# Stencil products over a chunk border by 32x32 corners, and another order of the first batches, in a four-layer kernel

## The chip, the cores and the metric

The kernel runs on one core of a Trainium2 chip. The metric is the device time of one execution in microseconds. A core has TensorE (PE; its weight loads are shown apart as PEld), VectorE (DVE), ScalarE (ACT), GpSimd (POOL) and SyncE (SP), which here only issues transfers. Each works through its own list of instructions in order and waits at semaphores for the others. Matmuls write to PSUM, which has eight banks of 128 rows x 512 f32; all else lives in SBUF, with 128 rows (partitions). A dimension of 256 is held as two chunks of 128 rows.

## The reference

Sixteen batches of a 256 x 256 array x pass through four layers, all f32.

```python
# 0: adapter with an expert chosen per batch, then layer norm
h = gelu(x @ down_W.T + down_b); h = h @ Wsel.T + bsel + emb
x = LN(h @ up_W.T + up_b + x) * gamma + beta
# 1: attention with 16 heads under a bias, a mask, a timestep's scale and shift; then a feed-forward
h = LN(x) * (1 + scale) + shift
x = h + softmax(q k^T / 4 + bias, mask) v @ Wo + bo
x = x + gelu2(LN2(x) @ W1 + b1) @ W2 + b2
# 2: one of three small networks, chosen per batch, then layer norm
x = LN(x + branch(x)) * gamma + beta
# 3: one step of a differential equation on the 256 x 256 grid
df = -(grad(A0*x, 1) + grad(A1*x, 2)) \
     + 0.5*(grad2(B0*x, 1) + grad2(B1*x, 2) + 2*grad(grad(B2*x, 2), 1))
x = max(x + df * dt, 0)
```

(The shift, scale and normalisations are as written in the usual way; the two mixed terms of layer 3 are equal.) `grad` is a central difference, `grad2` a second difference, each one-sided at the two outer rows or columns. So as a 256 x 256 matrix each has entries beside its diagonal and a few more in its first and last row.

## The kernel before

Everything of a batch stays on the chip from its first load to the output. The program is written out for all 16 batches, with no loop on the device, as nine generators ("chains"): `adapt` (layer 0, two batches at a time), `prepare` (its layer norms), `project` (q, k, v), `weigh` (scores and exponentials), `attend`, `enter` and `feed` (feed-forward), `end` (layer 2) and `step` (layer 3).

A planner, `Flow`, decides in which order their instructions are put into the engines' lists. A chain yields the time at which it can go on, or a condition on what other chains have done. `Flow` keeps a clock for each engine from fixed costs (`flow.pe(1.35)` adds 1.35 us to TensorE's), and takes, of the chains that are ready, the one with the lowest due time. A chain's due time begins at the number given to `flow.add` and grows with the TensorE time that it spends. The costs and due times only set the order: on the chip only semaphores count. Seven PSUM banks are shared among all chains (`misc` takes one, `free` gives it back), one is kept for the attention's context.

**Layer 3** (`step`). For a batch, `f` is the normalised array and `e_t` its transpose in PSUM. DVE and POOL multiply them by the grids: `b2_`, `a1`, `b1_` from the transpose, `a0`, `b0` from `f`. `e_z` is the first difference of `b2_` along the columns and is added to `a0`. Then `e_d` sums five products, for one output chunk `c` after the other, each in a bank of its own: the second difference along rows, `h_m` times `b0` (line 1128, two full matmuls, one for each chunk `k` of rows); the differences along columns of `a1` and `b1_` (line 1131, four matmuls of 129 columns, since from a chunk the matrices reach only one column beyond it); and the first difference along rows, `g_m` times `a0` (line 1135, two full matmuls). DVE then makes `f + dt * e_d` (line 1137), ACT applies the maximum (line 1145), SP stores. Matrices `g_m` and `h_m` hold the differences. For `k` other than `c`, only the entries next to the border between the two chunks are not zero: a corner of the 128 x 128 block.

**The start.** Constants are loaded from ACT's queue (`load`), the first inputs from SP's. Pair 0 passes `adapt`: `p_h` (line 543), Gelu to `a_h` (line 547), `p_e` with the expert's weights `e_w` (line 558), `p_u` (line 574) and the addition to `x` (line 580). POOL has first spread the mask (line 382) and added a bias to `x` (`biased`, line 529). `prepare` takes statistics (lines 417 to 425, on DVE and POOL), normalises, takes statistics again, and normalises once more to `c_ln` (line 433). `project` transposes `c_ln` to `c_t`, scales it on ACT and computes q, k and v with `w_qkv` (lines 646 and 689). `weigh` begins with the mask's product (line 733). `idle` (line 222) puts matmuls of zeros where TensorE has nothing else to do.

Of the kernel before, what the change touches and what calls it, by code (L numbers as in the profile page):

```python
# [170 lines left out]
def chain_kernel(ctx: ExitStack, tc: tile.TileContext, t: dict, out: bass.AP):  # L171
# [19 lines left out]
    def chunked(w):  # L191
        return w.rearrange("(k p) n -> p k n", p=P)
# [173 lines left out]

    rows_a = load("rows_a", rows(t["rows_a"]), [P, 5 * D])
    ln0_g, ln0_b, bv, bo, up_b = (rows_a[:, i * D : (i + 1) * D] for i in range(5))
    w_qkv = load("w_qkv", chunked(t["W_qkv"]), [P, NC, 3 * D])
    wq, wk, wv = (w_qkv[:, :, i * D : (i + 1) * D] for i in range(3))  # L370
    bqz = fixed("bqz", [P, NC])
    nc.vector.tensor_scalar(bqz, bq, columns("odd"), None, ALU.mult)
# [160 lines left out]
    def adapt():  # L533

        for p in range(B // 2):
            yield lambda: p in e_ws
            yield arrives.get(("t", p), 0.0)
            parts = [slice(i * A, (i + 1) * A) for i in range(2)]
            w, xt = e_ws.pop(p), xts.pop(p)
            ps_h = misc(f"p_h{p}", [2 * A, S])  # L540
            for k in range(NC):
                for i in range(2):
                    nc.tensor.matmul(
                        ps_h[parts[i]], w_down[:, k, :], xt[:, i, k, :], start=k == 0, stop=k == NC - 1
                    )
            h1 = xp.tile([2 * A, S], F32, name=f"a_h1{p}", tag="a_h1", bufs=1)
            nc.scalar.activation(h1, ps_h, AF.Gelu, bias=columns("down_b"))
            at = free(f"p_h{p}", flow.act(0.47, flow.pe(1.0), "gelu"))
            if p == 0:
                expert_bias()  # L550
            yield at
            if p == 0:
                spread_mask(0)
                for b in range(2):
                    biased(b)
            ps_e = misc(f"p_e{p}", [2 * A, S])
            for i in range(2):
                nc.tensor.matmul(ps_e[parts[i]], w[parts[i]], h1[parts[i]], start=True, stop=True)
            h2 = xp.tile([2 * A, S], F32, name=f"a_h2{p}", tag="a_h2", bufs=1)
            nc.vector.tensor_scalar(h2, ps_e, e_add[:, p : p + 1], None, ALU.add)  # L560
            at = free(f"p_e{p}", flow.dve(0.4, flow.pe(0.5)))
            if p and 2 * p + 2 < B:
                load_turned(p + 1)
                load_expert(p + 1)
            if p:
                yield lambda: ("x", 2 * p + 1) in done
            yield at, 2
            if p == 0:
                timestep()
                idle(256)  # L570
            ps_u = [misc(f"p_u{2 * p + i}", [P, NC, D]) for i in range(2)]
            for c in range(NC):
                for i in range(2):
                    nc.tensor.matmul(
                        ps_u[i][:, c, :], h2[parts[i], c * P : (c + 1) * P], up[parts[i]], start=True, stop=True
                    )
            at = flow.pe(1.0)
            for b in (2 * p, 2 * p + 1):
                x = xs[b]
                nc.vector.tensor_tensor(x, ps_u[b % 2], x, ALU.add)  # L580
                adapted[b] = free(f"p_u{b}", flow.dve(0.7, at))
                done.add(("adapt", b))
                yield 0.0, 0

    def prepare():
        for b in range(B):
            yield lambda: ("adapt", b) in done
            x, at = xs.pop(b), adapted.pop(b)
            yield at, 0
            flow.spent += 0.75  # L590
            if b + 2 < B:
                load_x(b + 2)
                if b == 0:
                    load_turned(1)
                    load_expert(1)
            if b == 1:
                choose()
            stat, at = take_stats(f"0_{b}", x, at)
            if b == 0:
                condition()  # L600
                idle(512, 512)
            yield at, 0
            tmp = xp.tile([P, NC, D], F32, name=f"b_tmp{b}", tag="b_tmp", bufs=1)
            at = normalized_affine(x, x, stat, ln0_g, ln0_b, tmp, b == 0)
            yield at, 0
            stat, at = take_stats(f"1_{b}", x, at)
            if b == 0:
                conditioned()
                masked.update((m, 0.0) for m in range(4))
            yield at, 0  # L610
            if b > 1:
                yield lambda: ("turned", b - 2) in done
            ln = xp.tile([P, NC, D], F32, name=f"c_ln{b}", tag="c_ln", bufs=2)
            lns[b] = ln, normalized(ln, x, stat, b == 0)
            flow.spent += 1.5
            if b + 2 < B:
                biased(b + 2)
            done.add(("normal", b))

    def project():  # L620
# [464 lines left out]
    def step():  # L1085
# [6 lines left out]
        for b in range(B):  # L1092
            yield lambda: ("branch", b) in done
            y, stat, at = stats3.pop(b)
            yield at, 0
            tmp = wide(f"e_tmp{b}")
            f = y
            yield normalized_affine(f, y, stat, ln3_g, ln3_b, tmp, b == B - 1)
            ps_t = misc(f"e_t{b}", [P, NC, S])
            at = transposed(ps_t, f)  # L1100
            b2_, a1, b1_ = (wide(f"e_{n}{b}") for n in ("b2", "a1", "b1"))
            for dst, grid in ((b2_, b2_g), (a1, a1_g), (b1_, b1_g)):
                nc.vector.tensor_tensor(dst, ps_t, grid, ALU.mult)  # L1103
                at = flow.dve(0.6, at)
            free(f"e_t{b}", at)
            a0, b0 = wide(f"e_a0{b}"), wide(f"e_b0{b}")
            nc.gpsimd.tensor_tensor(a0, f, a0_g, ALU.mult)
            nc.gpsimd.tensor_tensor(b0, f, b0_g, ALU.mult)
            flow.pool(2.7)
            yield at - 1.4  # L1110
            ps_z = misc(f"e_z{b}", [P, NC, S])
            for c in range(NC):
                rng = slice(c * P, (c + 1) * P)
                nc.tensor.matmul(ps_z[:, c, :], b2_[:, 0, rng], g_m[:, 0, :], start=True, stop=False)  # L1114
                nc.tensor.matmul(  # L1115
                    ps_z[:, c, reach[1]], b2_[:, 1, rng], g_m[:, 1, reach[1]], start=False, stop=True
                )
            at = flow.pe(1.35)
            nc.vector.tensor_tensor(a0, ps_z, a0, ALU.add)
            yield free(f"e_z{b}", flow.dve(0.61, at))  # L1120
            if b == B - 2:
                yield lambda: ("branch", B - 1) in done
            o = wide(f"e_o{b}")
            for c in range(NC):
                rng = slice(c * P, (c + 1) * P)
                ps_d = misc(f"e_d{b}_{c}", [P, S])
                for k in range(NC):
                    nc.tensor.matmul(ps_d, h_m[:, k, rng], b0[:, k, :], start=k == 0, stop=False)  # L1128
                for k in range(NC):
                    for src, w in ((a1, g_m), (b1_, h_m)):  # L1130
                        nc.tensor.matmul(  # L1131
                            ps_d[:, reach[k]], src[:, k, rng], w[:, k, reach[k]], start=False, stop=False
                        )
                for k in range(NC):
                    nc.tensor.matmul(ps_d, g_m[:, k, rng], a0[:, k, :], start=False, stop=k == NC - 1)  # L1135
                at = flow.pe(2.6)
                nc.vector.scalar_tensor_tensor(  # L1137
                    o[:, c, :], ps_d, dt[:, b : b + 1], f[:, c, :], ALU.mult, ALU.add
                )
                at = free(f"e_d{b}_{c}", flow.dve(0.4, at))  # L1140
                part = slice(c, c + 1) if b == B - 1 else slice(0, NC)
                if c:
                    done.add(("step", b))
                if c or b == B - 1:
                    nc.scalar.activation(o[:, part, :], o[:, part, :], AF.Relu)  # L1145
                    flow.act(0.54, at)
                    nc.sync.dma_start(
                        out=out[b].rearrange("(c p) d -> p c d", p=P)[:, part, :], in_=o[:, part, :]
                    )
                yield 0.0  # L1150

    flow.add(adapt(), -3.55, 1.2)
    flow.add(prepare(), -2.34, 2.25)
    flow.add(project(), -0.88, 5.7)
    flow.add(weigh(), 0, 21.2)
    flow.add(attend(), 0.96, 11.3)
    flow.add(enter(), -0.11, 0.44)
    flow.add(feed(), 2.45, 13.9)
    flow.add(end(), 2.86, 3.95)
    flow.add(step(), 4.31, 7.0)  # L1160
    flow.run()

def _arrays(inputs):
# [79 lines left out]
```

## Time and profile before

| | |
|---|---|
| median of three runs | 924.78 us (921.94 to 926.36) |
| profiled execution | 923.92 us, its span 922.1 us |
| TensorE busy | 882.4 us (96%), mean granted clock 0.978 |
| DVE, ACT, POOL busy | 627.8, 556.5, 376.6 us |
| first scores on TensorE | 41.39 us |
| last matmul of batch 15's e_d ends | 918.4 us |

A profile line of the timeline gives the start, the length, the engine, the line of the kernel, the operation, what it writes and reads, its shape, and how many records are merged ("x4"); in brackets the idle time of the engine before it and what ended it. "128*128 128x256" is a matmul that uses 128 rows and 128 columns of the array and writes 128 x 256 elements. Matmuls overlap, so the spacing of their starts says what one costs, and not their length. One f32 matmul leaves two records.

### The profile page before, as it was taken

To read this page: it belongs to the slowest core of one execution; us is meant where nothing else is said; L and a number is where in the kernel's file an instruction comes from. 1 tells how busy PE (TensorE), PEld (TensorE's weight loads), DVE (VectorE), ACT (ScalarE), POOL (GpSimd) and SP (SyncE) were. 2 spreads that over 40 slices of the span, in tenths; PEclk is the share of its full clock that TensorE was granted. 3 is DMA by queue.
4 is the path that set the end of the run, shared out by engine and by line. 5 is a ranking of instruction groups with operands and counts; after the bars stand their busy time and mean duration, and the time that the engine had idled before them with its cause. 6 is when DMAs were issued, how large, how long until landed. Compare 5 with 4: busy or idle time off the path is not lost. (4 is left out here: it accounts for less than half of the span.)

```text
span 922.1 us, 18224 instructions
## 1 busy us (share of the span) xinstructions
PE 882.4 (96%) x6180; PEld 692.1 (75%) x6180; DVE 627.8 (68%) x2078; ACT 556.5 (60%) x1561; POOL 376.6 (41%) x514
## 2 busy tenths in 40 slices
PE   7799898999999999999999999999999999999997
PEld 4467585778787787877787778877878778877785
DVE  4477766888576777766767666766777676766443
ACT  2376747766566666766675767666675655656320
POOL 2234526653522425344543636154452525222331
PEclk7699999999999999999999999999999999999999
DMA  9269978876777877778667776777667775850010
GB/s 296 72 218 296 288 190 211 223 186 175 182 195 189 218 178 188 202 182 213 161 181 210 192 184 178 188 187 193 155 183 180 181 200 143 220 135 29 13 41 23
DMA packets 130972, 163.25 MB, mean 177 GB/s; under 512 B 12713, under 2 KB 94779, under 8 KB 130875
## 3 DMA queue, kind: packets, MB, share of 16 engines
q1 hardware_dynamic: 97920, 96.92, 33.1%
q0 software_dynamic: 31680, 62.92, 33.0%
q10 hardware_dynamic: 1275, 2.19, 0.7%
q8 instruction: 52, 0.85, 0.4%
q14 instruction: 45, 0.37, 0.1%
HBM read 94.89 MB, written 4.19 MB: 107 GB/s over the span
## 5 line engine op out<-in xcount | busy, mean ns | idle before, releaser
L767 ACT ACTIVATE c_pr<-c_sc,c_mx 128x256 f32<-128x256 f32 x512 | 254.9, 500 | 165.8 <-DVE c_mx L756 164.7
L756 DVE CUSTOM_DVE_ANT_0 c_sc<-c_s,side 128x256 f32<-128x256 f32 x512 | 193.6, 418 | 34.7 <-PE c_s L738 18.0
L464 PE MATMUL c_pt<-ident,c_pr 128*128 128x128 f32 x1024 | 143.5, 278 | 6.7 <-DVE x L580 2.1
L464 PEld LDWEIGHTS c_pt<-ident,c_pr 128*128 128x128 f32 x1024 | 116.8, 142 | 34.2 <-issue 11.9
L472 DVE COPY c_pts<-c_pt 128x512 f32<-128x512 f32 x175 | 117.2, 685 | 26.8 <-PE c_pt L464 26.5
L922 PE MATMUL d_f<-d_ht,w 128*128 128x256 f32 x512 | 122.3, 382 | 0.4
L421 POOL TENSOR_SCALAR rs<-mv 128x2 f32<-128x2 f32 x64 | 14.2, 222 | 253.2 <-DVE mv L418 252.7
L952 PE MATMUL d_o<-w,d_z 128*128 128x256 f32 x512 | 115.9, 380 | 0.1
L517 POOL DMA_DIRECT2D side<-neg x60 | 80.7, 1345 | 59.5 <-DMA side<-in_side 20.8
L952 PEld LDWEIGHTS d_o<-w,d_z 128*128 128x128 f32 x512 | 94.9, 190 | 12.5 <-DVE c_mx L756 0.6
L922 PEld LDWEIGHTS d_f<-d_ht,w 128*128 128x128 f32 x512 | 92.8, 190 | 15.1 <-issue 2.5
L767 ACT ACTIVATION_READ_ACCUMULATOR c_pr<-c_sc,c_mx 128x1 f32 x512 | 96.3, 188 | 0.0
L738 PE MATMUL c_s<-c_kt,c_qz 32*128 32x256 f32 x1024 | 78.3, 401 | 4.2 <-DVE c_mx L756 3.8
L821 PE MATMUL c_c<-c_pts,c_va 128*32 128x256 f32 x1024 | 72.6, 385 | 2.5 <-ACT c_pts L474 1.8
L738 PEld LDWEIGHTS c_s<-c_kt,c_qz 32*128 32x128 f32 x1024 | 49.1, 184 | 25.2 <-issue 12.2
L474 ACT COPY c_pts<-c_pt 128x512 f32<-128x512 f32 x81 | 45.5, 575 | 21.1 <-PE c_pt L464 21.0
L941 ACT ACTIVATE d_f<-d_z 128x512 f32<-128x512 f32 x64 | 38.4, 600 | 28.3 <-DVE d_z L938 27.2
L821 PEld LDWEIGHTS c_c<-c_pts,c_va 128*32 128x32 f32 x1024 | 27.9, 109 | 35.0 <-issue 18.2
L456 POOL TENSOR_TENSOR b_tmp<-b_tmp,rows_a 128x512 f32<-128x512 f32 x15 | 19.6, 1304 | 84.1 <-DVE b_tmp L433 65.7
L938 DVE TENSOR_SCALAR d_z<-d_f,cols 128x256 f32<-128x256 f32 x88 | 38.5, 479 | 17.3 <-PE d_f L922 17.2
L422 POOL TENSOR_TENSOR rs<-rs,inv_sqrt 128x2 f32<-128x2 f32 x64 | 46.0, 718 | 5.3
L960 DVE SCALAR_TENSOR_TENSOR y<-d_o,y 128x256 f32<-128x256 f32 x32 | 13.6, 424 | 45.4 <-PE d_o L952 45.4
(152 smaller groups left out, 1606.6 us busy)
## 6 DMA issues: line engine op xcount, KB each, us to landing
side<-in_side SPq DMA_DIRECT2D x256, 256.0 KB, 5.3
side<-neg POOLq DMA_DIRECT2D x60, 1024.0 KB, 8.1
d_w<-in_W_branch SPq DMA_DIRECT2D x16, 512.0 KB, 4.4
xt<-in_x_t SPq DMA_DIRECT2D x16, 256.0 KB, 5.2
x<-in_x SPq DMA_DIRECT2D x16, 256.0 KB, 5.9
out<-e_o SPq DMA_DIRECT2D x15, 256.0 KB, 3.9
w<-in_W SPq DMA_DIRECT2D x2, 1024.0 KB, 7.0
d_bout<-in_bl_branch SPq DMA_DIRECT2D x16, 128.0 KB, 4.3
```

What stands on the lines that cost most here:

```text
L422: nc.gpsimd.tensor_tensor(rs, rs, inv_sqrt, ALU.pow)
L464: nc.tensor.transpose(ps[:, k, c * P : (c + 1) * P], src[:, c, k * P : (k + 1) * P], ident)
L472: nc.vector.tensor_copy(dst, ps)
L474: nc.scalar.copy(dst, ps)
L517: nc.gpsimd.dma_start(out=sides[m].rearrange("p (h c) k -> p h (c k)", h=HB), in_=negs[m // 4].rearrange("p c k -> p (c k)").unsqueeze(1). ...
L738: nc.tensor.matmul(ps[i][:, c, :], qz[rows32, par, half, c * P : (c + 1) * P], k_t[rows32, half, :], start=b > 0, stop=b > 0 or c == NC - 1,)
L756: nc.vector.tensor_tensor_reduce(out=sc[:, c, :], in0=ps[i][:, c, :], in1=sb[:, i * NC + c, :], scale=-1.0, scalar=3.0e38, op0=ALU.add, op ...
L767: nc.scalar.activation(pr[:, c, :], sc[:, c, :], AF.Exp, bias=mx[:, c : c + 1], scale=-1.0, accum_out=sums[:, c, h : h + 1],)
L821: nc.tensor.matmul(ps_c[32 * i : 32 * i + 32, :], va[:, k, 4 * half + i, 2 * par : 2 * par + 2, :].rearrange("p e d -> p (e d)"), turned[i ...
L922: nc.tensor.matmul(ps_f[:, i, :], w1[:, k, f * P : (f + 1) * P], h_t[:, k, :], start=k == 0, stop=k == NC - 1,)
L938: nc.vector.tensor_scalar(z[:, i, :], ps_f[:, i, :], b1[:, f : f + 1], None, ALU.add)
L952: nc.tensor.matmul(ps_o, us[f // 2][:, f % 2, c * P : (c + 1) * P], w2[:, f, :], start=f == 0, stop=f == NF - 1,)
```

## The change

In `step`, the two output chunks share one bank `ps_d`. The first step sums what does not depend on `e_z`: each chunk's own block of `h_m` times `b0`, and the differences along columns. After a yield the second step adds four corner products (`next_to`: the last 32 rows of one chunk against the first 32 of the other, a 32 x 32 piece of the array), and each chunk's own block of `g_m` times `a0`. One DVE instruction then takes both chunks; for the last batch, one for each chunk, both behind the last matmul.

In the setup, `w_qkv` is loaded behind the first Gelu on ACT's queue. Pair 1 and later pairs of `adapt` wait for batch 1's last normalisation, and the addition to batch 1's `x` waits for batch 0's. The biases of batches 1 and 2 are added after batch 0's normalisation; batch 0's comes before the mask is spread. The third group of `idle` has four matmuls for two. The planner gets new costs for `step` and new due times.

```diff
-    w_qkv = load("w_qkv", chunked(t["W_qkv"]), [P, NC, 3 * D])
+    w_qkv = fixed("w_qkv", [P, NC, 3 * D])
...
-            yield lambda: p in e_ws
+            yield lambda: p in e_ws and (p == 0 or ("normal", 1) in done)
...
             if p == 0:
+                nc.scalar.dma_start(out=w_qkv, in_=chunked(t["W_qkv"]))
                 expert_bias()
             yield at
             if p == 0:
+                biased(0)
                 spread_mask(0)
-                for b in range(2):
-                    biased(b)
...
             for b in (2 * p, 2 * p + 1):
+                if b == 1:
+                    yield lambda: ("normal", 0) in done
                 x = xs[b]
...
-                idle(512, 512)
+                idle(512, 512, 512, 512)
...
-            if b + 2 < B:
-                biased(b + 2)
+            for n in (1, 2) if b == 0 else (b + 2,) if b + 2 < B else ():
+                biased(n)
...
-            yield free(f"e_z{b}", flow.dve(0.61, at))
+            at_z = free(f"e_z{b}", flow.dve(0.61, at))
+            yield 0.0
             if b == B - 2:
                 yield lambda: ("branch", B - 1) in done
             o = wide(f"e_o{b}")
-            for c in range(NC):
+            ps_d = misc(f"e_d{b}", [P, NC, S])
+            def own(w, src, c, start=False, stop=False):
                 rng = slice(c * P, (c + 1) * P)
-                ps_d = misc(f"e_d{b}_{c}", [P, S])
-                for k in range(NC):
-                    nc.tensor.matmul(ps_d, h_m[:, k, rng], b0[:, k, :], start=k == 0, stop=False)
+                nc.tensor.matmul(ps_d[:, c, :], w[:, c, rng], src[:, c, :], start=start, stop=stop)
+            def next_to(w, src, c):
+                near, far = slice(0, 32), slice(P - 32, P)
+                at, of = (near, far) if c else (far, near)
+                rng = slice(c * P + at.start, c * P + at.stop)
+                nc.tensor.matmul(
+                    ps_d[at, c, :], w[of, 1 - c, rng], src[of, 1 - c, :], start=False, stop=False
+                )
+            for c in range(NC):
+                own(h_m, b0, c, start=c == 0)
+            for c in range(NC):
+                rng = slice(c * P, (c + 1) * P)
                 for k in range(NC):
                     for src, w in ((a1, g_m), (b1_, h_m)):
...
-                for k in range(NC):
-                    nc.tensor.matmul(ps_d, g_m[:, k, rng], a0[:, k, :], start=False, stop=k == NC - 1)
-                at = flow.pe(2.6)
+            flow.pe(2.65)
+            yield at_z
+            for w, src in ((h_m, b0), (g_m, a0)):
+                for c in range(NC):
+                    next_to(w, src, c)
+            for c in range(NC):
+                own(g_m, a0, c, stop=c == NC - 1)
+            at = flow.pe(1.6)
+            for part in [slice(c, c + 1) for c in range(NC)] if b == B - 1 else [slice(0, NC)]:
                 nc.vector.scalar_tensor_tensor(
-                    o[:, c, :], ps_d, dt[:, b : b + 1], f[:, c, :], ALU.mult, ALU.add
+                    o[:, part, :], ps_d[:, part, :], dt[:, b : b + 1], f[:, part, :], ALU.mult, ALU.add
                 )
...
-    flow.add(adapt(), -3.55, 1.2)
+    flow.add(adapt(), -3.31, 1.2)
     flow.add(prepare(), -2.34, 2.25)
-    flow.add(project(), -0.88, 5.7)
+    flow.add(project(), -0.45, 5.7)
     flow.add(weigh(), 0, 21.2)
-    flow.add(attend(), 0.96, 11.3)
-    flow.add(enter(), -0.11, 0.44)
-    flow.add(feed(), 2.45, 13.9)
-    flow.add(end(), 2.86, 3.95)
-    flow.add(step(), 4.31, 7.0)
+    flow.add(attend(), 0.9, 11.3)
+    flow.add(enter(), -0.18, 0.44)
+    flow.add(feed(), 2.55, 13.9)
+    flow.add(end(), 3.08, 3.95)
+    flow.add(step(), 4.65, 7.0)
```

More of the change, by code (lines that the diff above doesn't have):

```diff
@@ L1131, in step @@
                         nc.tensor.matmul(
-                            ps_d[:, reach[k]], src[:, k, rng], w[:, k, reach[k]], start=False, stop=False
-                        )
-                for k in range(NC):
-                    nc.tensor.matmul(ps_d, g_m[:, k, rng], a0[:, k, :], start=False, stop=k == NC - 1)
-                at = flow.pe(2.6)
+                            ps_d[:, c, reach[k]],
+                            src[:, k, rng],
+                            w[:, k, reach[k]],
+                            start=False,
@@ L1137, in step @@
+                            stop=False,
+                        )
+            flow.pe(2.65)
[7 more added lines that the diff above has]
+            for part in [slice(c, c + 1) for c in range(NC)] if b == B - 1 else [slice(0, NC)]:
                 nc.vector.scalar_tensor_tensor(
-                    o[:, c, :], ps_d, dt[:, b : b + 1], f[:, c, :], ALU.mult, ALU.add
+                    o[:, part, :], ps_d[:, part, :], dt[:, b : b + 1], f[:, part, :], ALU.mult, ALU.add
@@ L1139, in step @@
                 )
[L1140 to L1149, printed above, removed]
@@ L1150, in step @@
-                yield 0.0
-    flow.add(adapt(), -3.55, 1.2)
+                at = flow.dve(0.75, at)
+                nc.scalar.activation(o[:, part, :], o[:, part, :], AF.Relu)
+                flow.act(0.54, at)
+                nc.sync.dma_start(out=out[b].rearrange("(c p) d -> p c d", p=P)[:, part, :], in_=o[:, part, :])
+            free(f"e_d{b}", at)
+            done.add(("step", b))
+    flow.add(adapt(), -3.31, 1.2)
     flow.add(prepare(), -2.34, 2.25)
-    flow.add(project(), -0.88, 5.7)
+    flow.add(project(), -0.45, 5.7)
```

## The prediction

> **What bounds the kernel now.** I read the page first, then busy time stage by stage, then the timeline of the start, of two places in steady state, and the chain at the end.
>
> ```profile
> PE 882.4 (96%) x6180; PEld 692.1 (75%) x6180; DVE 627.8 (68%) x2078; ACT 556.5 (60%) x1561; POOL 376.6 (41%) x514
> ```
>
> Stage by stage (stretch, its length, then busy time of PE, PEld, DVE, ACT, POOL, granted clock, DMA share, GB/s):
>
> ```profile
> 25.00:32.00 7.00, 4.59 (x16) 2.18 (x16) 1.58 (x7) 0.47 (x1) 2.24 (x4) 0.50 0.32 94
> 32.00:43.00 11.00, 10.35 (x46) 8.04 (x49) 4.38 (x18) 5.13 (x9) 2.59 (x5) 0.67 0.12 33
> ...
> 300.00:500.00 200.00, 196.77 (x1438) 156.21 (x1437) 145.56 (x479) 133.14 (x375) 89.00 (x116) 1.00 0.75 193
> 500.00:700.00 200.00, 198.64 (x1449) 159.24 (x1448) 139.73 (x468) 136.36 (x381) 90.75 (x124) 1.00 0.73 184
> ```
>
> From 43 us on TensorE is the bound: it stands still for 4.6 us of 400 there, while DVE and ACT are at 70%. So TensorE time removed in steady state moves the end one for one. Before 43 us it is no bound: it runs at half clock and waits. Two places matter, one per half of the change.
>
> **The differences (e_d), steady state.** The timeline of TensorE, in start, length, instruction:
>
> ```profile
> 204.88 1.07 PE L821 MATMUL c_c<-c_pts,c_va 128*32 128x256 f32 x16
> 205.88 1.99 PE L1069 MATMUL d_y<-d_w,d_hid 128*128 128x256 f32 x8
> ...
> 211.85 0.39 PE L1131 MATMUL e_d<-grids,e_a 128*128 128x129 f32 x2
> 212.07 0.39 PE L1131 MATMUL e_d<-grids,e_b 128*128 128x129 f32 x2
> 212.29 1.03 PE L1135 MATMUL e_d<-e_a,grids 128*128 128x256 f32 x4
> 213.16 0.60 PE L464 MATMUL c_pt<-ident,c_pr 128*128 128x128 f32 x4
> ```
>
> One f32 matmul leaves two records. Four of 256 columns start at 212.29 and the next tile starts at 213.16: 0.87 us, so 0.43 for a matmul of 256 columns. A 129-column one takes 212.07 - 211.85 = 0.22. One batch's e_d is 8 x 0.43 + 8 x 0.22 = 5.2 us; the chain at the end agrees (901.14 to 906.39).
>
> Removed: the four full matmuls that take one chunk of rows into the other, 4 x 0.43 = **1.73 us** per batch. Added: four 32x32 corners of 256 columns. No 32x32 row exists. The nearest is p_e: two 64x64 matmuls on diagonal corners, both into one bank.
>
> ```profile
> 607.90 0.65 PE L558 MATMUL p_e<-a_h,e_w 64*64 64x256 f32 x4
> ```
>
> Four records end within 0.65, where the four of L1135 show 1.03; read one by one they start at 607.902, 607.908, 608.168 and 608.175, so both corners run at once. Here the Trainium skill speaks against the change: TensorEngine Tiling (Array Packing), section Restrictions and Gotchas, says that different row tiles cannot access the same PSUM bank at one time, and both corners of a pair come from different row groups and write into the one bank of e_d. By the rule the four corners go one after another, 1.73 us, and nothing is gained; by the p_e row two pairs take the time of two matmuls. I go by the row: same bank, different rows, no serialisation in this trace.
>
> The price of leaving and re-entering the whole array is in the c_c rows: 16 records in four rounds (each of four column tiles at once) take 205.88 - 204.88 = 1.00 where four rounds of 0.216 are 0.86. Behind it d_y's eight records show 1.99 where other groups of eight show 1.89: its second weight load is no longer hidden, 0.10. Read one by one, the first record of a tiled block starts 0.309 behind a 256-column record instead of 0.216: 0.09 more. The corners are also four rounds (two pairs, two records each), so 1.00 + 0.10 + 0.09 = 1.19, and the saving is 1.73 - 1.19 = **0.54 us per batch**. Ends: with only one switch to pay, beside another tiled block, 0.95 (saving 0.78); all serial plus switches, 1.73 + 0.29 = 2.02 (loss 0.29). Over 16 batches -12.5 to +4.6, taken at -8.6 before the end is looked at.
>
> The rest of step is hidden. One bank held through both steps replaces two held in turn. One 128x512 addition (0.69, as L1119 has) replaces two of 0.48 on a DVE that is 70% busy; if that cover were gone it is still no loss. The second step's wait for e_z is covered by the first (2.6 us of matmuls against 0.7 of DVE), as it was.
>
> **The end** is not hidden. Its chain in order of time:
>
> ```profile
> 904.62 0.89 PE e_d L1131 x8
> 905.51 0.88 PE e_d L1135 x4
> 906.39 0.02 issue
> 906.42 0.48 DVE e_o L1137
> 906.90 0.40 DVE e_tmp L447
> ```
>
> Batch 15's normalisation (e_tmp) is queued on DVE behind batch 14's e_o, which waits for its matmuls. These end 0.54 sooner, but the addition is 0.69 instead of 0.48: -0.3. For batch 15, matmuls -0.54, but both chunks now end together and the second addition waits for the first, +0.41: -0.1. So 14 x 0.54 + 0.4 = **8.0 us** for this half.
>
> **The start.** Timeline of the first 48 us:
>
> ```profile
> 17.40 0.69 DVE L580 TENSOR_TENSOR x<-p_u,x 128x512 f32<-128x512 f32 x1 [2.42 <-PE p_u L574]
> ...
> 18.91 0.69 DVE L580 TENSOR_TENSOR x<-p_u,x 128x512 f32<-128x512 f32 x1 [0.82 <-POOL x L529]
> ...
> 20.66 3.76 PE L222 MATMUL idle<-c_va 128*128 128x512 f32 x4
> ...
> 30.32 0.48 DVE L560 TENSOR_SCALAR a_h<-p_e,e_add 128x256 f32<-128x256 f32 x1 [5.49 <-PE p_e L558]
> 30.72 0.73 DVE L433 TENSOR_SCALAR c_ln<-x,mv,rs 128x256 f32<-128x256 f32 x2
> ...
> 33.06 3.78 PE L646 MATMUL c_q<-c_xt,w_qkv 128*128 128x256 f32 x8 [0.66 <-ACT c_xt L632]
> ...
> 41.39 1.04 PE L733 MATMUL c_s<-neg,ident_b 128*128 128x256 bf16 x8
> ```
>
> Batch 0's c_ln needs only rs, which POOL has at 25.6, but stands on DVE behind pair 1's a_h, which waits for pair 1's inputs. Holding pair 1 back until both first batches are normalised takes a_h away. Step by step:
> - x of batch 1 no longer stands before batch 0's statistics: they start at 17.40 + 0.69 = 18.1 instead of 19.52.
> - From there to rs took 25.6 - 19.5 = 6.1, so c_ln is possible at 24.2, not 30.72.
> - TensorE is not free then: ps_a ends at 20.66, and the idle matmuls are now eight records. They start 0.853 apart at half clock, 6.8 us, to 27.5. The skill (TensorE: Matmul & The Clock Gate, Part 1) gives the full clock after a busy window of about 3.4 us. The row seems to contradict it: 3.76 us of idle matmuls at 0.50 throughout. But the granted clock changes on a grid of 3.41 us (22.19 to 25.60 is one window), and the row ends inside it at 24.4. The longer block fills that window. By the rule the clock is full from 25.6 and the block ends at 26.5; by the row alone at 27.5 and everything behind it stays at half. I take the rule: c_t at 26.5.
> - c_t to c_q took 1.9, at full clock 1.5: c_q at 28.0. q, k and v are 24 records of 0.216, 5.2 us, so the first scores stand at 33.2 instead of 41.39. One window of 3.4 us back at half clock, as the gaps around c_t may cause, costs 1.7. Between: 34.0, **-7.4**.
> - Pair 1's work (p_h, p_e), done in the old gap, now falls into the full stage: four pair rounds and two, with switches about **+2.0**.
>
> Net -5.4. By the row alone (half clock to the end, c_t at 27.5, then the old 10.2 to the scores at 37.7, +2.0) it is -1.7. At best the second e_w, for which p_e waits until 13.03, lands up to 2.4 us sooner, since w_qkv (768 KB at some 330 GB/s) no longer runs ahead of it: -8. I take **-5**.
>
> What I cost at nothing: w_qkv is issued after the first Gelu (about 10.3) instead of 7.0; its 5.8 us to landing makes 16, under contention 20, and c_q needs it at 28, so 8 us of cover. The issue itself (0.39) delays Sin and Tanh behind it on ACT's queue; silu came at 15.0 and ps_a began at 17.23. SP issues in the old order. On POOL biased(0) now precedes the mask: x is there by 13.2 and the mask needs to be spread only by 33. biased(1) and biased(2) move behind batch 0's statistics on POOL, to about 24.5 and 25.8; queued behind them is batch 1's rs, and batch 1's x on DVE waits for biased(1). Batch 1 had its statistics at 33.67, so it has 7 us. Pair 1's x is needed for batch 2, whose c_t stands at 71.43, some 30 us behind the place of pair 1's new turn.
>
> The planner's costs and due times change too, so the order of everything is dealt anew. I cannot derive it. TensorE is idle 24 us between 43 and 900, so about +-5 bounds it; taken at 0.
>
> **Sum.** The profiled execution took 923.92 (span 922.1 and 1.8 around it): 923.9 - 8.0 - 5.0 = 910.9. The median of the runs is 0.9 above it, so **911.8**.
>
> **Rivals.**
> - Corners one after another (the PSUM rule): +4.6 for the differences and -5 for the start: 924. The p_e row speaks against it; that no 32x32 row and no anti-diagonal pair is in the trace speaks for it. 0.10.
> - The start gives nothing, since the stage behind it waits for other things instead: 924.8 - 8.0 = 916.8. For it: from 70 to 120 us the DMA share is 1.04. Against it: between 43 and 120 us TensorE is idle 7 of 77 us, and DVE waits 0.8 us in all for a transfer. 0.15.
> - The new order eats about half of the gain: 921. 0.06.
> - Slower: the corners' price alone. If each of their eight records is a round of its own with a drain between (0.216 + 0.09), a block is 2.45 plus 0.10, and 0.82 x 16 = +13, less 5: 933. It decides from a block of 1.73 + 5/16 = 2.04 us, and passes 0.5% at 1.73 + 9.6/16 = 2.33. Against it: tiled blocks in this trace pay only at their ends. 0.08.
> - A miss of both signs that I haven't named: 0.03.
>
> **Chances.** The likeliest has 0.58, its own range 906 to 917. Half a per cent (4.6 us) is what a measurement of this kernel can tell. Faster: 0.58 + 0.15 and 0.02 of the unnamed, 0.75. Same: 0.10 + 0.06, 0.16. Slower: 0.08 + 0.01, 0.09. The range reaches from both halves at their good ends (911.8 - 4.5 - 3 = 904) nearly to the serial corners, 923.
>
> **What would show it.** Right: e_d at 4.7 us per batch instead of 5.2; the corners' records starting in pairs some ns apart; c_ln near 24, the first scores near 34, clock at 1.00 from about 26. Wrong: corners 0.216 apart in single file; c_ln behind another wait on DVE or POOL; TensorE idle over 10 us between 43 and 120.

## The result and the profile after

| | before | after |
|---|---|---|
| median of the runs beside each other | 923.36 us (919.77 to 926.36, 4 runs) | 912.69 us (912.22 to 913.27, 4 runs) |
| profiled execution, its span | 923.92, 922.1 us | 912.22, 910.4 us |
| mean granted clock | 0.978 | 0.990 |

The ratio is 0.9902 (0.9873 to 0.993): 1% faster, at the predicted place. The first lines to read are the page's first row and the busy time by stage (length, PE, PEld, DVE, ACT, POOL, granted clock, DMA share, GB/s), of after:

```profile
PE 869.3 (95%) x6184; PEld 668.7 (73%) x6184; DVE 636.2 (70%) x2087; ACT 544.1 (60%) x1537; POOL 377.4 (41%) x514
```

```profile
25.00:32.00 7.00, 5.29 (x40) 4.08 (x39) 3.91 (x15) 2.84 (x8) 4.97 (x7) 1.00 0.45 132
32.00:43.00 11.00, 8.23 (x59) 5.23 (x57) 7.71 (x29) 8.04 (x20) 2.77 (x6) 0.84 0.31 97
300.00:500.00 200.00, 194.45 (x1419) 151.40 (x1421) 143.66 (x474) 132.51 (x375) 89.82 (x120) 1.00 0.76 192
500.00:700.00 200.00, 195.28 (x1434) 152.90 (x1431) 143.57 (x469) 125.70 (x355) 87.27 (x117) 1.00 0.70 176
```

TensorE is still the bound and 13 us less busy. The stretch 25 to 32 us, at half clock before, runs at full clock. But in steady state TensorE stands still for 10.3 us of 400, where it was 4.6. From batch 0's products with the keys to batch 15's d_y, a stretch of 857 us in both, it stands still for 26.7 us, and 23.9 before: other stretches stand still less.

**The differences.** The timeline of TensorE, of after (line numbers have moved: own blocks L1133, differences along columns L1149, corners L1139, addition L1165):

```profile
191.55 1.03 PE L1133 MATMUL e_d<-e_b,grids 128*128 128x256 f32 x4
...
193.98 0.39 PE L1149 MATMUL e_d<-grids,e_b 128*128 128x129 f32 x2
...
198.12 0.62 PE L1139 MATMUL e_d<-e_b,grids 32*32 32x256 f32 x4
198.58 0.60 PE L1139 MATMUL e_d<-e_a,grids 32*32 32x256 f32 x4
199.10 1.13 PE L1133 MATMUL e_d<-e_a,grids 128*128 128x256 f32 x4
200.07 0.59 PE L924 MATMUL d_f<-d_ht,w 128*128 128x256 f32 x2
```

All four corners lie between 198.12 and 199.10: 0.98 us where four full matmuls took 1.73. Read record by record, the eight starts of a block are 0, 7, 240, 247, 456, 463, 672 and 679 ns, within 1 ns in all sixteen batches: two corners on the anti-diagonal, in one bank, run at once. Entering costs 0.093 more, and behind the block the second record starts 0.320 after the first instead of 0.216, so the block costs 1.18. One batch's e_d is 4.69 instead of 5.24.

**The start**, timeline of TensorE and DVE, of after:

```profile
10.38 0.65 PE L558 MATMUL p_e<-a_h,e_w 64*64 64x256 f32 x4 [0.24 <-ACT a_h L547]
...
15.92 5.25 PE L222 MATMUL idle<-c_va 128*128 128x512 f32 x8
20.69 0.74 DVE L433 TENSOR_SCALAR c_ln<-x,mv,rs 128x256 f32<-128x256 f32 x2 [0.80 <-POOL rs L422]
21.16 0.87 PE L464 MATMUL c_t<-ident,c_ln 128*128 128x128 f32 x4
22.68 2.02 PE L648 MATMUL c_q<-c_xt,w_qkv 128*128 128x256 f32 x8 [0.65 <-ACT c_xt L634]
...
26.27 1.04 PE L735 MATMUL c_s<-neg,ident_b 128*128 128x256 bf16 x8
29.01 1.15 PE L740 MATMUL c_s<-c_kt,c_qz 32*128 32x256 f32 x16 [1.71 <-ACT c_kt L679]
```

c_ln, released by rs and no longer standing behind pair 1's a_h, comes at 20.69 (30.72 before). The mask's product, first of the scores, comes at 26.27 (41.39), the products with the keys at 29.01 (42.36). The scores of batches 1, 2 and 3 come 7.8, 10.7 and 6.8 us earlier.

**The end**, the chain that ended last, of after:

```profile
892.88 0.75 DVE e_o L1165
893.64 0.40 DVE e_tmp L447
...
896.92 1.22 PE e_z L1116 x2
...
899.86 1.71 PE e_d L1133 x4
901.57 2.61 PE e_d L1149 x16
904.18 0.98 PE e_d L1139 x8
905.16 1.07 PE e_d L1133 x4
...
906.78 0.81 ACT e_o L1169 x2
```

Batch 15's e_d takes 6.4 us instead of 5.3. Most of its first two lines ran at half clock (granted 0.50 from 896.3 to 903.2), which costs more than its corners save. Before, one window at 0.50 lay there, from 909.7 to 913.1, and ended ahead of batch 15's e_d (913.12).

### The profile page after: what moved, and what is told of

Its sections match the earlier page's. It is cut to its first block, busy times and chain, and to the rows that moved or that the text cites. A ratio compares the mean times of both kernels' runs of the same rounds, so it can differ in the third digit from the quotient of the medians.

```text
span 910.4 us, 18249 instructions
## 1 busy us (share of the span) xinstructions
PE 869.3 (95%) x6184; PEld 668.7 (73%) x6184; DVE 636.2 (70%) x2087; ACT 544.1 (60%) x1537; POOL 377.4 (41%) x514
## 5 line engine op out<-in xcount | busy, mean ns | idle before, releaser
L472 DVE COPY c_pts<-c_pt 128x512 f32<-128x512 f32 x206 | 137.0, 683 | 21.8 <-PE c_pt L464 21.2
L464 PEld LDWEIGHTS c_pt<-ident,c_pr 128*128 128x128 f32 x1024 | 114.3, 141 | 43.3 <-issue 14.5
L940 DVE TENSOR_SCALAR d_z<-d_f,cols 128x256 f32<-128x256 f32 x94 | 41.0, 477 | 16.2 <-PE d_f L924 16.0
L947 DVE SCALAR_TENSOR_TENSOR d_z<-d_f,d_z 128x512 f32<-128x512 f32 x64 | 43.4, 677 | 1.8 <-ACT d_f L943 1.8
L1029 POOL TENSOR_TENSOR y<-y,d_bout 128x256 f32<-128x256 f32 x32 | 23.6, 790 | 47.1 <-PE d_t L464 32.1
```

The lines of the kernel that those rows point to most:

```text
L464: nc.tensor.transpose(ps[:, k, c * P : (c + 1) * P], src[:, c, k * P : (k + 1) * P], ident)
L472: nc.vector.tensor_copy(dst, ps)
L940: nc.vector.tensor_scalar(z[:, i, :], ps_f[:, i, :], b1[:, f : f + 1], None, ALU.add)
L947: nc.vector.scalar_tensor_tensor(z, ps_f, 1.0, z, ALU.add, ALU.mult)
```

## The experiments

The theory: the differences save about 0.54 us per batch because pairs of corners overlap, the start is worth about 5 us, and the order of everything else is neutral. The rivals: the gain comes from the order or the start alone; w_qkv's later place is the start's cause; the pace of `step` in the planner matters. Times below are medians, each beside the kernel before in the same series; ratios are to it.

### One part alone

**e1_step_only**: the kernel before with the new `step` and its planner costs; start and due times as before.

```diff
-                ps_d = misc(f"e_d{b}_{c}", [P, S])
+            ps_d = misc(f"e_d{b}", [P, NC, S])
...
-                at = flow.pe(2.6)
+            flow.pe(2.65)
+            yield at_z
...
+            at = flow.pe(1.6)
```

> The kernel before with the new differences and their planner costs alone (old start, old due times). My theory, corners at 0.54 us a batch and 0.4 at the end: 923.4 - 8 = 915, with some us either way for the order, which shifts because the costs do. Rival, that the gain came from the start and the new order: 922 to 925. In either case a corner block should take 0.98 us and the first scores stay near 41 to 42 us.

937.55 us, ratio 1.0162 (1.0121 to 1.0203): slower by 15 us. e_d is shorter as in after (77.9 us in all, from the start of each record to the next, 87.3 before). But the new costs made the planner deal another order, and TensorE's idle time from batch 0's products with the keys to batch 15's d_y rose from 23.9 to 38.0 us. In this section that stretch is meant wherever idle time is given.

**e2_start_only**: after, with `step` and all due times of before; so everything of the start is in it. Behind the start the order is that of before, but for pair 1's work.

```diff
-            ps_d = misc(f"e_d{b}", [P, NC, S])
+                ps_d = misc(f"e_d{b}_{c}", [P, S])
...
-    flow.add(step(), 4.65, 7.0)
+    flow.add(step(), 4.31, 7.0)
```

> The kernel before with the new start alone (w_qkv later, pair 1 held back, biases moved, four idle matmuls); the order behind the start stays nearly that of before. My theory: first scores near 29 us as in the changed kernel, 13 us earlier, but with pair 1's 2 us moved behind and the rest given back between 30 and 120 us, the end gains 5: 918. Rival A, nothing of it arrives: 923. Rival B, all of it less pair 1's work arrives: 923.4 - 11 = 912.

917.06 us (14 runs), ratio 0.9946 (0.992 to 0.9971): the start is worth 5.0 us, 2.7 to 7.4. The first products with the keys, on the timeline of TensorE, in before and then in this run:

```profile
42.36 1.15 PE L738 MATMUL c_s<-c_kt,c_qz 32*128 32x256 f32 x16
```

```profile
29.46 1.15 PE L740 MATMUL c_s<-c_kt,c_qz 32*128 32x256 f32 x16
```

They come 12.9 us earlier, but batch 1's scores 10.5, batch 2's 8.2, batch 3's 6.4, and from there it stays at 6.4 to 6.8. The 14 runs fall into two groups, six from 912.69 to 914.4 and eight from 916.95 to 919.78; the profiled one (914.01) is of the lower.

**e3_dues_only**: the kernel before with the seven changed due times alone.

```diff
-    flow.add(adapt(), -3.55, 1.2)
+    flow.add(adapt(), -3.31, 1.2)
...
-    flow.add(step(), 4.31, 7.0)
+    flow.add(step(), 4.65, 7.0)
```

> The kernel before with the new due times alone. My theory, the order is a shuffle worth 0 within 5 us: 923 (918 to 928). Rival, the due times carry a part of the gain: below 918.

946.55 us, ratio 1.027 (1.0225 to 1.0314): 25 us lost although no instruction is added or removed. Waits of TensorE, of this run (us in all, times, the longest):

```profile
PE c_pt L464 <- ACT c_pr L767: 6.2, 10, 2.4
PE c_pt L464 <- DVE c_mx L756: 4.6, 5, 1.2
```

In before these two are 1.3 us (2 times) and 0.8 us (2 times): the probabilities' transposes now stand too early for the engines that feed them. Idle time is 39.5 us, 15.6 more than in before. The rest of the 25 us is busy time: the same groups take longer in this order, the transposes c_pt 5.1 us and the scores' products 3.4.

### The corners alone, in the order of after

**e4_full_blocks**: after, with each corner widened to the full block. The order on every engine is that of after.

```diff
-                near, far = slice(0, 32), slice(P - 32, P)
-                at, of = (near, far) if c else (far, near)
-                rng = slice(c * P + at.start, c * P + at.stop)
-                nc.tensor.matmul(
-                    ps_d[at, c, :], w[of, 1 - c, rng], src[of, 1 - c, :], start=False, stop=False
-                )
+                rng = slice(c * P, (c + 1) * P)
+                nc.tensor.matmul(ps_d[:, c, :], w[:, 1 - c, rng], src[:, 1 - c, :], start=False, stop=False)
```

> The changed kernel with each corner replaced by the full 128x128 block, in the very same order on every engine. My theory, a corner block with its switches is 1.18 us and four full matmuls 1.73: 14 x 0.55 + 1 = 8.5 more, 912.7 + 8.5 = 921. Rival, TensorE is not the bound behind the start, so that its time is worth less than one for one: 915 to 918. Rival, the switches eat the corners' gain: 912.7.

922.93 us, ratio 1.0015 (0.999 to 1.0039). Against after's 0.9902, measured in another series, the corners are worth 0.0113, 10.4 us, with about 3.5 either way from the two intervals. The timeline of TensorE shows the four full products from 200.72 to 202.44, 1.72 us where the corners took 0.98:

```profile
200.72 1.03 PE L1137 MATMUL e_d<-e_b,grids 128*128 128x256 f32 x4
201.58 1.03 PE L1137 MATMUL e_d<-e_a,grids 128*128 128x256 f32 x4
202.44 1.03 PE L1133 MATMUL e_d<-e_a,grids 128*128 128x256 f32 x4
203.31 1.89 PE L924 MATMUL d_f<-d_ht,w 128*128 128x256 f32 x8
```

e_d takes 87.75 us in all, after's 78.1: 9.6 less. In the same series this kernel is 5.9 us slower than e2, with about 3 either way, from which it differs only in `step`'s two steps in one bank, `step`'s planner costs, the due times and the order that follows from them. So that is the price of the new order, two steps included, when the corners are left out. After has the same order, so it should pay it too.

### What makes the start faster

**e5_qkv_early**: after, with w_qkv loaded in its old place.

```diff
-    w_qkv = fixed("w_qkv", [P, NC, 3 * D])
+    w_qkv = load("w_qkv", chunked(t["W_qkv"]), [P, NC, 3 * D])
...
-                nc.scalar.dma_start(out=w_qkv, in_=chunked(t["W_qkv"]))
```

> The changed kernel with w_qkv loaded where it was before, in the same order on every engine otherwise. My theory, w_qkv ahead of the second e_w is what kept p_e until 13.0 and let the clock fall: p_e is back at 13, TensorE at half clock to 25 or so, c_ln at 24, q at 26 to 28, the first scores 6 to 8 us later than now; some of it is absorbed later, so the end is 2 to 4 later, 915 to 917. Rival, the place of w_qkv is indifferent and holding pair 1 back did it all: p_e at 10.4 and 912.7.

916.8 us, ratio 0.9952 (0.993 to 0.9973); after was 4.1 us faster by the medians, 4.6 by the ratios with about 3 either way. Timeline of TensorE, of this run:

```profile
11.80 0.61 PE L557 MATMUL p_e<-a_h,e_w 64*64 64x256 f32 x2 [2.34 <-DMA e_w<-in_expert_W]
13.92 0.97 PE L557 MATMUL p_e<-a_h,e_w 64*64 64x256 f32 x2 [1.50 <-DMA e_w<-in_expert_W]
...
27.63 2.02 PE L647 MATMUL c_q<-c_xt,w_qkv 128*128 128x256 f32 x8 [0.66 <-ACT c_xt L633]
...
33.76 1.15 PE L739 MATMUL c_s<-c_kt,c_qz 32*128 32x256 f32 x16 [1.51 <-ACT c_kt L678]
```

p_e waits for e_w and starts 1.4 and 3.5 us after the 10.38 of after, and the products with the keys come 4.75 us later, 33.76 for 29.01. The two loads stand in different queues: e_w's two parts are issued from SP's at 6.25 and about 7.6, w_qkv from ACT's at 6.94. From issue to landing the parts of e_w take 5.4 and 6.2 us here, 2.1 and 3.3 in after, and the DMA share from 8 to 10 us is 0.93 here and 0.59 in after. So a transfer that is needed late slowed one that is needed first.

**e9_qkv_late_only**: the kernel before, with w_qkv loaded late and nothing else.

```diff
-    w_qkv = load("w_qkv", chunked(t["W_qkv"]), [P, NC, 3 * D])
+    w_qkv = fixed("w_qkv", [P, NC, 3 * D])
...
+                nc.scalar.dma_start(out=w_qkv, in_=chunked(t["W_qkv"]))
```

> The kernel before with one edit: w_qkv loaded behind the first Gelu; everything else in the order of before. The prediction's step held that pair 1 standing ahead of c_ln was the cost of the start and that w_qkv's place gives at best 2.4: 920 to 922, c_ln still near 28 to 30 us behind pair 1's a_h. Rival, after the run with w_qkv early (4.1 slower than the changed kernel): w_qkv's place is most of the start's gain, p_e at 10.4, clock up, and the end 4 sooner, 918.

923.4 us, ratio 1.0031 (1.0014 to 1.0048): no gain, rather a loss of 1 to 4 us. The timeline of TensorE and DVE, of this run:

```profile
10.57 0.65 PE L559 MATMUL p_e<-a_h,e_w 64*64 64x256 f32 x4 [0.24 <-ACT a_h L547]
...
27.02 2.73 PE L543 MATMUL p_h<-xt,w_down 128*64 128x256 f32 x8 [6.39 <-DMA xt<-in_x_t]
30.31 1.12 PE L559 MATMUL p_e<-a_h,e_w 64*64 64x256 f32 x4 [0.57 <-ACT a_h L547]
31.50 0.48 DVE L561 TENSOR_SCALAR a_h<-p_e,e_add 128x256 f32<-128x256 f32 x1 [5.54 <-PE p_e L559]
31.90 0.73 DVE L433 TENSOR_SCALAR c_ln<-x,mv,rs 128x256 f32<-128x256 f32 x2
```

p_e is nearly as early as in after, but c_ln still stands behind pair 1's a_h, which waits for pair 1's inputs. The early e_w without holding pair 1 back gives nothing, and holding pair 1 back without the early e_w (e5) leaves 4.1 us unused. What holding back gives by itself in the order of before wasn't run.

**e6_idle_two**: after, with two idle matmuls instead of four in the third group.

```diff
-                idle(512, 512, 512, 512)
+                idle(512, 512)
```

> The changed kernel with two idle matmuls instead of four ahead of batch 0's c_t, same order. Theory, the longer block keeps or brings the full clock for q and k: without it 16.0 to 21.2 is not filled, q and k run at half clock and the first scores come 2 to 4 us later; at the end 0 to 2 later, 913 to 915. Rival, with p_e at 10.4 the clock is up by itself: no change, 912.7.

913.16 us, ratio 0.9912 (0.9884 to 0.9939), beside after's 0.9902: no difference. The timeline of TensorE, of this run:

```profile
22.69 3.59 PE L648 MATMUL c_q<-c_xt,w_qkv 128*128 128x256 f32 x8 [0.66 <-ACT c_xt L634]
...
29.02 1.15 PE L740 MATMUL c_s<-c_kt,c_qz 32*128 32x256 f32 x16
```

c_q takes 3.59 us here, since the clock is at 0.50 from 22.5 to 26.0, where after's c_q takes 2.02. Yet the products with the keys come at 29.02, in after at 29.01, where TensorE waited 1.71 for ACT's c_kt: the slower c_q only fills that wait. So the clock of c_q, on which the prediction spent a page's rule, decides nothing.

### The end, and a faster kernel

**e7_tail_warm**: after, with matmuls of zeros into a bank that nobody reads, ahead of batch 15's transposes and behind them.

```diff
+            if b == B - 1:
+                idle(512, 512, 512)
             ps_t = misc(f"e_t{b}", [P, NC, S])
             at = transposed(ps_t, f)
+            if b == B - 1:
+                idle(256)
```

> The changed kernel with idle matmuls at its end, three of 512 columns before batch 15's e_t and one of 256 behind it; same order otherwise. Theory, the end lost to the clock: e_z and half of batch 15's e_d ran at 0.50 from 896.3 to 903.2, since TensorE stood between 892.8 and 896.9; filled, the clock stays up and the end comes 3 us sooner, 909.6. Rival, the idle matmuls delay e_t and cost what they gain: 912 to 914.

910.8 us (909.95 to 911.78), ratio 0.9886 (0.9859 to 0.9914): the lowest of all kernels here, 1.9 us under after, though the two intervals overlap. The chain at the end, of this run:

```profile
897.64 0.70 PE e_z L1120 x2
...
899.22 0.87 PE e_d L1137 x4
900.09 1.79 PE e_d L1153 x16
901.88 0.98 PE e_d L1143 x8
902.86 1.07 PE e_d L1137 x4
```

e_z's first pair takes 0.70 for 1.22, e_d's first two lines 2.66 for 4.32. From batch 15's d_y to the end it is 21.3 us, 24.3 in after and 23.0 in before.

### The order

**e8_own_pace**: after's start and `step`, the due times of before, and `step`'s pace set to its own cost.

```diff
-    flow.add(step(), 4.65, 7.0)
+    flow.add(step(), 4.31, 6.04)
```

(The other due times as in before.)

> New start, new differences, old due times, but the due time of step paced by its own new cost (divided by 6.04 instead of 7.0). Theory, the loss of 15.6 with the new differences alone came because step's due time grew by 0.86 a batch, so that it overtook the other chains and pushed the scores back; at its own pace that is gone, and start (-4.9) and corners (-10) arrive in full: 922 - 15 = 907 to 910. Rival, any other order costs some 20 us, whatever the pace: 925 to 935.

933.38 us, ratio 1.0136 (1.0105 to 1.0166). The theory that `step` runs too far ahead, since each batch advances its due time by 7.0 for a cost of 6.04, fell. TensorE's idle time is 40.6 us.

**e10_same_order**: e2 with the new `step`; the planner is told the old costs, so that each engine's order is that of e2. Both chunks' products stand where the second chunk's were.

```diff
+            n = flow.take()
+            flow.free_at[n] = flow.dve(0.4, flow.pe(2.6))
+            yield 0.0
             ps_d = misc(f"e_d{b}", [P, NC, S])
```

> New start and new differences with the planner told the old costs and due times, so that every engine keeps the order of the run with the new start alone (917.1); the products of both chunks stand together in the place of the second chunk. Theory, start and corners add up and only the new order took 5 back: 917.1 less 8 to 10 = 907 to 909, below the changed kernel's 912.7. Rival, the corners are worth less in this order (TensorE not bound): 912 to 916.

**e11_corners_old_order**: the same `step` in the kernel before, with the start of before.

```diff
-                ps_d = misc(f"e_d{b}_{c}", [P, S])
+            ps_d = misc(f"e_d{b}", [P, NC, S])
```

> The kernel before with the new differences alone, the planner told the old costs, so that the order is that of before. Theory, corners 8 to 10 faster than before: 922 - 9 = 913, and the 937.6 of the new differences with their new costs was all order, 24 us of it. Rival, the differences as written (one bank, second step, one addition) cost by themselves: 925 to 938.

**e12_same_order_warm**: e10 with the idle matmuls of e7 at the end.

```diff
+                idle(512, 512, 512)
...
+                idle(256)
```

> The run with the same order and both halves, with idle matmuls of zeros at the end (three of 512 columns before batch 15's e_t, one of 256 behind it). Theory, the clock of the last products stays up as it did in the changed kernel (910.8 for 912.7): 2 below the run without, 905 to 907. Rival, in this order the clock doesn't fall at the end, and it is the same within 1.

| | median | ratio |
|---|---|---|
| e10 | 923.58 us (20 runs) | 1.0025 (1.001 to 1.004) |
| e11 | 928.52 us (9 runs) | 1.0084 (1.0057 to 1.011) |
| e12 | 920.86 us (20 runs) | 1.0004 (0.9989 to 1.0019) |

e12 confirms the warm end (2.7 us under e10 by the medians, 1.9 by the ratios). The other two miss by about 15 us. e_d is 8.6 us shorter in e10 than in e2, but the scores' products are 10.8 us longer (96.3 for 85.5, from start to next start). Eight of the 64 groups make up 10.3 of it. One of them, on the timeline, in e2 (TensorE) and then in e10 (with its weight loads and DVE):

```profile
476.78 1.03 PE L1137 MATMUL e_d<-e_a,grids 128*128 128x256 f32 x4
477.74 1.15 PE L740 MATMUL c_s<-c_kt,c_qz 32*128 32x256 f32 x16
```

```profile
479.36 0.60 PE L464 MATMUL c_pt<-ident,c_pr 128*128 128x128 f32 x4
479.89 2.02 PE L740 MATMUL c_s<-c_kt,c_qz 32*128 32x256 f32 x16
480.05 0.69 DVE L472 COPY c_pts<-c_pt 128x512 f32<-128x512 f32 x1
480.79 0.19 PEld L740 LDWEIGHTS c_s<-c_kt,c_qz 32*128 32x128 f32 x2 [0.31 <-DVE c_pts L472]
```

In e2 the first chunk's e_d (2.6 us) stands ahead of the scores, and they start in fours, 7 ns apart. In e10 that work is in the second slot, so TensorE arrives at the scores 2.6 us earlier beside the other engines. One group's four products each need a bank, and the third and fourth begin at 480.79, as soon as DVE has read c_pts out of its bank. In e11 too the scores' products are 10.8 us longer than in before (94.6 for 83.8). So these two kernels test the corners together with a lost cover of 2.6 us, as far as this group shows it, and are no clean test of the corners; e4 beside after is.

## Why the prediction was right, and where its steps were off

912.69 us was measured where 911.8 was predicted, and e4 and e2 confirm both halves, about 10 and 5 us. That the time came out within 1 us is luck. As a gain it is further off: 13.0 us was forecast (924.8 to 911.8), and 10.7 came by the medians, 9.0 by the ratio (6.5 to 11.7), for beside it the kernel before ran at 923.36 and not at 924.8. Steps that were off in both directions cancel in part.

- **The corners, 1.19 us a block, 8.0 us for the half.** Right. The block is 1.18, e_d falls from 5.24 to 4.69 (0.55; 0.54 predicted). e4 beside after gives 10.4 with 3.5 either way, which takes in the 8.0. That holds in the order of after alone: in the kernels with the corners in another order (e1, e8, e10, e11) other losses outweigh them. The p_e row was the right one to go by. The rule from the Trainium skill that was weighed against it (TensorEngine Tiling (Array Packing), Restrictions and Gotchas: no two row tiles in the same PSUM bank at one time) does not hold for these pairs, which start 6 to 7 ns apart. The rival with corners one after another fell, and so did that with a drain for each. The rival in which the start gives nothing fell with e2.
- **The start, -5.** The size is right (e2: -5.0), but two of its terms are not, and their errors cancel. "Between: 34.0, -7.4" was off: the first scores came at 26.27, 15.1 earlier than before. The step at fault is "at best the second e_w ... lands up to 2.4 us sooner", named as the good end only; e5 measures w_qkv's place at 4.1. "Pair 1's work ... about +2.0" was right for that work: in e2, its p_h, p_e and p_u take 2.0 us more between the first scores and batch 3's. But in the same stretch another 4.5 us are lost, mostly at c_s, c_pt and c_c (1.8, 1.4 and 1.1 us more with the idle time behind them), for which the prediction's sum had no term. The lead of 12.9 us shrinks to 6.4, which is nearly where -5.4 had put it.
- **The clock of the start.** The block of eight idle matmuls ran as the prediction took from the Trainium skill's TensorE: Matmul & The Clock Gate (half clock from 15.7 to 19.1, then full). It decided nothing (e6).
- **The order, "about +-5 bounds it; taken at 0".** This step failed. The bound was argued from TensorE's 24 us of idle time, but idle time can also grow. It is 23.9 us in before, 25.2 in e2, 26.7 in after and in e4, but 38.0, 39.5 and 40.6 in e1, e3 and e8: an order that isn't fitted to its instructions costs 14 to 16 us of idle time (e1 and e3 beside before, e8 beside e2). Nor does idle time bound it, since in e3 busy time grew too. For after's order the term is +5.9 (e4 beside e2, with 3 either way), at the edge of the bound and not 0. The rival in which the new order eats about half of the gain came nearest to this: it ate 5.9 of 15.4. How the 5.9 divides stays open. Between the two traces, whose executions lie 10.2 us apart, 3.6 is the stretch from batch 15's d_y to the end, in which the clock was at 1.00 in e2 and fell in e4, and 1.6 is idle time ahead of it; the rest wasn't separated.
- **The end, -0.3 and -0.1.** Batch 14's e_d and its longer addition went as worked out (e_d 4.71 for 5.25, the addition 0.75 for 0.48). Batch 15's was missed: +1.1 on TensorE instead of -0.54, because two windows at half clock in a row (896.3 to 903.2) reach into it; e7 and e12 take back 2 to 3 us. The second addition's wait is there as predicted (ACT 0.81 for 0.42).
- **The sum of the parts.** Predicted were 5.0 for the start, 8.0 for the corners and 0 for the order. Start 5.0 and corners 10.4 make 15.4, and the order took back 5.9: 9.5. That this agrees with 9.0 by the ratio is no check, since before, e2, e4 and after are one path of three steps.

## What to carry to other kernels

Before a piece of the array is dismissed for its switches, read from a row of like shape how much the tiles overlap, and add the entry and the first unhidden weight load once per block, not per matmul. In a kernel whose order is dealt by a planner, an edit of costs or due times alone can cost more than the edit of the instructions gains; test the instructions in one fixed order (e4) and the order with one set of instructions (e3), and don't take an edit's value from a kernel whose order was dealt for other work. Look at the granted clock of the last microseconds: where the last chain waits for other engines, a few matmuls of zeros gave about 2 us here (e7, e12).

## What the runs showed of the hardware

Two 32x32 corners on the anti-diagonal, from different rows of the array into different rows of one PSUM bank, start 6 to 7 ns apart and cost 0.216 us per round of 256 columns like one full record; the tile view of after holds for all 16 batches (duration in ns, minimum/median/maximum):

```profile
L1139 PE MATMUL e_d<-e_b,grids x64: 374/386/398, 198.1 to 904.4; 32*32 32x256 f32 x64
L1139 PE MATMUL e_d<-e_a,grids x64: 374/374/374, 198.6 to 904.8; 32*32 32x256 f32 x64
```

Entering costs a tiled block 0.09 us, leaving it 0.09 (0.311 from the last round to the next full record), and the second full record behind it comes 0.10 late (0.320 for 0.216). In the traces the granted clock changes in windows of 3.41 us or multiples of it (19.1 - 15.7, 39.6 - 36.2, 903.2 - 896.3). Row tiles need not stay together: in seven groups of the scores in e10 the starts of neighbouring rows spread from 7 ns to between 0.2 and 1.2 us, and groups that took 1.08 to 1.27 us in e2 took 1.9 to 3.9; in the one shown above, a bank was late.
